# Transposes of two rows at once in even rows, strip transposes in odd rows, and the norm parameters in the transposes' PSUM banks

## The chip, the cores and the metric

The kernel runs on one core of a Trainium2 chip. The metric is the device time of one execution in microseconds. Before the change it was 2425.87 us, the median of three runs from 2424.24 to 2426.8.

## What is computed

The input is x, 8 images of 256 channels and 56 x 56 points, in fp32. There are two layers, each a block on a group norm of its input, added to that input:

```
# layer 0: involution
g   = group_norm(x)                                 # 32 groups of 8 channels
ker = w_span @ (w_reduce @ g + b_reduce) + b_span   # 16 groups x 49 taps per point
x   = x + sum over 49 taps of ker * patches7x7(g)   # 16 channels share a group's taps
# layer 1: two 3x3 convolutions with ternary weights, batch norms and relus
h   = relu(bn(conv(group_norm(x), tern(w1)) + centre term))
x   = x + relu(h + bn(conv(h, tern(w2)) + centre term))
```

The change lies in layer 0 alone.

## The kernel before

The program has four stretches: the involution, two convolutions (the function `conv_phase`, called twice) and a last pass that adds everything up. The involution is the function's part under `ph1`.

An image is cut into four **quarters** of 64 channels; the two halves of the partitions hold the upper and lower half of the image. A quarter has ten **rows** (`TY`), each of seven blocks of 3 x 8 points per half. The main loop (L811) goes over 32 quarters and the ten rows in each; `r = c * TY + ty` counts the 40 rows of an image.

TensorE does this in a row:

- `apply_row` (L690) multiplies patches by the quarter's tap matrices `a`: 56 matmuls into a PSUM tile `pa`. The patches are in a tile `q`, transposed, so that the points of a block lie on the partitions. Four of the seven block columns of `q` come by DMA from a DRAM buffer `xtd`, loaded four rows ahead by `prefetch`; three are made on the chip.
- `transpose_q` (L634) makes these three: three transposes from the padded image `xe` into a PSUM tile `ptq`, and a copy by ScalarE into `q` (L641). It runs two rows ahead (`QLEAD`).
- `generate` (L650) makes the next quarter's matrices in 14 **units**, one or two per row as `PER_ROW` says, none in the last row. A unit's matmuls `pg` go into a PSUM tile, ScalarE takes some of its planes (L675) and VectorE the rest (L680) into `a`.
- In every second row of a part of the image, `prep` (L582) makes a **strip** of the next image: GpSimd normalizes and spreads it into `xn` (L561), four transposes go into a PSUM tile `pt` (L605), ScalarE copies it to `stg` (L608), and DMAs store it to `xtd`. There are 16 strips per image. `xn` is one buffer.
- From row 20 on, `params` (L466) turns the next image's statistics into scale and shift: a matmul `gnp` with the group matrix (L146), a short chain on VectorE, a second matmul (L155), a longer chain with a square root on ScalarE (L158 to L161), and 16 small matmuls `br` (L478). It is a generator; the loop calls it once per row, and each `yield` ends a step.

`pick_out` (L710) then takes a row's result out of `pa`: ScalarE (L716), VectorE (L717), and GpSimd adds it to x (L720). VectorE also takes statistics of finished rows.

[...] The tag `ps`, two tiles of two banks, serves the units, the reduction `pk` (L538) and the parameters. The tags `pt` (transposes of both kinds) and `pa` have two tiles of one bank each. A tile goes back to its tag when its last reader is done.

The order of work on each engine is that of the program text: `pin` (L753) ties each instruction in the loop to the one before it on its engine. So a wait of one instruction holds up everything behind it on that engine. `transfer(2)` at the head of a row issues the strip's stores that are in `tasks`.

Of the kernel before, what the change touches and what calls it, by code (L numbers as in the profile page):

```python
# [7 lines left out]
F32 = mybir.dt.float32  # L8
# [7 lines left out]
P = 128  # L16
# [3 lines left out]
K, PAD, G = 7, 3, 16  # L20
KK = K * K
CR = C // 4
# [4 lines left out]
CH = P // 2  # L27
NCQ = C // CH
GQ = G // NCQ
GP = GQ // 2  # L30
HH = H // 2
# [3 lines left out]
TY, TX = 10, W // PX  # L35
# [15 lines left out]
SR = HH // 4  # L51
NSP = SR * QX
# [7 lines left out]
QLEAD = 2  # L60
# [18 lines left out]
def involution_tri_block_kernel(  # L79
# [3 lines left out]
    nc = tc.nc  # L83
# [57 lines left out]
    def group_norm_params(mv, dst, psum_tile, name):  # L141


        n = mv.shape[1]
        ps = psum_tile(f"gnp_{name}")
        nc.tensor.matmul(ps[:, :2 * n], grp_sb, mv.rearrange("p n s -> p (n s)"),  # L146
                         start=True, stop=True)
        yield
        gm = small.tile([P, n, 2], F32, tag=f"gn_gm{n}", name=f"gm_{name}")
        nc.vector.tensor_copy(gm.rearrange("p n s -> p (n s)"), ps[:, :2 * n])  # L150
        d = small.tile([P, n], F32, tag=f"gn_d{n}", name=f"d_{name}")
        nc.vector.tensor_tensor(d, mv[:, :, 0], gm[:, :, 0], ALU.subtract)
        nc.vector.tensor_tensor(d, d, d, ALU.mult)
        ps2 = psum_tile(f"gnp2_{name}")
        nc.tensor.matmul(ps2[:, :n], grp_sb, d, start=True, stop=True)  # L155
        yield
        var = small.tile([P, n], F32, tag=f"gn_var{n}", name=f"var_{name}")
        nc.vector.tensor_tensor(var, ps2[:, :n], gm[:, :, 1], ALU.add)  # L158
        rs = rstd_of(var, GN_EPS, name)
        nc.vector.tensor_copy(dst[:, :, 0], rs)  # L160
        nc.vector.scalar_tensor_tensor(dst[:, :, 1], gm[:, :, 0], -1.0, rs, ALU.mult, ALU.mult)  # L161
# [273 lines left out]
    with ExitStack() as ph1:  # L435
        ps_p = ph1.enter_context(tc.tile_pool(name="ps_p", bufs=2, space=PSUM))
        ps_a = ph1.enter_context(tc.tile_pool(name="ps_a", bufs=2, space=PSUM))

        def ps_tile(name):
            return ps_p.tile([P, 2, 512], F32, tag="ps", name=name)  # L440

        def ps_flat(name):
            return ps_tile(name).rearrange("p a f -> p (a f)")

# [21 lines left out]
        def params(b):  # L466


            dst = small.tile([P, NCQ, 2], F32, tag="gn1", name=f"gn1_{b}")
            yield from group_norm_params(mvs.pop(b), dst, ps_flat, f"a{b}")  # L470
            ps = ps_flat(f"br_{b}")
            for c in range(NCQ):
                nc.vector.tensor_scalar(
                    wrn[:, c, :].rearrange("p (i r) -> p i r", i=2),
                    wr[:, c, :].unsqueeze(1).to_broadcast([P, 2, CR]),
                    dst[:, c, 0:1], None, ALU.mult)
                for i in range(2):
                    nc.tensor.matmul(ps[i * CR:(i + 1) * CR, :1], wr[:CH, c, :], dst[:CH, c, 1:2],  # L478
                                     start=(c == 0), stop=(c == NCQ - 1))

            edge = small.tile([P, 2, NCQ], F32, tag="gn1e", name=f"gn1e_{b}")
            for j in range(2):
                nc.vector.tensor_scalar(edge[:, j], dst[:, :, 1], side_sb[:, j:j + 1], None, ALU.mult)
            prm[b], prm_edge[b] = dst, edge
            yield
            nc.vector.tensor_tensor(brn, br, ps[:, :1], ALU.add)

        gst1, mvs = {}, {}
# [13 lines left out]
        wr, wrn = fixed([P, NCQ, CR], "wr"), fixed([P, NCQ, 2 * CR], "wrn")  # L502
# [18 lines left out]
        for d in (d for ds in xt_d for d in ds):  # L521
            for r0, n in ((0, PAD), (PAD + HH, HQ - PAD - HH)):
                e = n * QX * RP // P
# [58 lines left out]
        def prep(b):  # L582

            for c in range(NCQ):
                d = xt_d[b % 2][c][:]

                def store(src, row, o=None, d=d):

                    n = src.shape[0]
                    if o is None:
                        src, to = src.rearrange("p k c -> p (k c)"), [[1, RP]]
                    else:
                        to = [[P, NK], [1, CH]]
                    nc.sync.dma_start(
                        bass.AP(d.tensor, d.offset + row * QX * RP + (o or 0), [[RP, n]] + to), src)

                for s in range(HH // SR):
                    spread(xn, xs[b, c][:, s * SR * W:(s + 1) * SR * W], 0, NK,  # L600
                           prm[b][:, c, 0:1], prm[b][:, c, 1:2])
                    yield
                    pt = ps_a.tile([P, 512], F32, tag="pt", name=f"pt_{b}_{c}_{s}")
                    for k in range(NK):
                        nc.tensor.transpose(pt[:NSP, k * P:(k + 1) * P],  # L605
                                            xn[:, k].rearrange("p r x -> p (r x)"), ident_sb)
                    stg = work.tile([P, NK, P], F32, tag="stg", name=f"stg_{b}_{c}_{s}")
                    nc.scalar.copy(stg[:NSP].rearrange("p k c -> p (k c)"), pt[:NSP, :RP])  # L608
                    tasks.append(lambda stg=stg, s=s: store(stg[:NSP], PAD + s * SR))

                    e = PAD * QX
                    if s == 0:
                        tasks.append(lambda stg=stg: store(stg[:e, :, CH:], PAD + HH, 0))
                    elif s == HH // SR - 1:
                        tasks.append(lambda stg=stg: store(stg[NSP - e:NSP, :, :CH], 0, CH))
                    yield


        tasks = []

        def transfer(n=1):
            while tasks and n:
                tasks.pop(0)()
                n -= 1
# [8 lines left out]

        def transpose_q(b, c, ty):  # L634

            pt = ps_a.tile([P, 512], F32, tag="pt", name=f"ptq_{b}_{c}_{ty}")
            for k in range(NX):
                nc.tensor.transpose(  # L638
                    pt[:NQ, k * P:(k + 1) * P],
                    xe[c % 2][:, k, PY * ty:PY * ty + QY].rearrange("p r x -> p (r x)"), ident_sb)  # L640
            nc.scalar.copy(loads[b, c, ty][:NQ, NK:].rearrange("p k c -> p (k c)"),  # L641
                           pt[:NQ, :NX * P])
# [134 lines left out]
            reduce(0, py)  # L777
        for _ in prep(0):
            transfer(len(tasks))
        apool = ph1.enter_context(tc.tile_pool(name="apool", bufs=1))  # L780

        def matrices(m):
# [14 lines left out]


        X_AT = (0, 1, 4, 5, 7, 8, 14, 15)
        STRIPS_AT = 23  # L800
        for _ in range(NQB):
            prefetch()
        for _ in surround(0, 0):
# [1 line left out]
        rows = [(b, c, ty) for b, c in quarters for ty in range(TY)]  # L805
        for k in rows[:QLEAD]:
            transpose_q(*k)
        pin(start=True)
        last = None
        strips = iter(())  # L810
        for m, (b, c) in enumerate(quarters):  # L811
            a = a_next
            gen = iter(())
            if m + 1 < len(quarters):
                a_next = matrices(m + 1)
                gen = generate(*quarters[m + 1], a_next)
                around = surround(*quarters[m + 1])
            more = b + 1 < B
            for ty in range(TY):
                r = c * TY + ty  # L820

                if last is not None and ty in (2, 3):
                    store_x1(*last, ty - 2)
                elif more and r in X_AT:
                    load_x(b + 1, X_AT.index(r) // 2, X_AT.index(r) % 2)
                transfer(2)

                row = apply_row(b, c, a, ty)
                prefetch()
                if m * TY + ty + QLEAD < len(rows):  # L830
                    transpose_q(*rows[m * TY + ty + QLEAD])

                if more and r >= 20:
                    if r == 20:
                        norm = params(b + 1)
                    next(norm, None)
                if ty == 1 and last is not None:
                    gn2_stats(*last, TY)
                elif ty >= 2:
                    gn2_stats(b, c, ty - 1)  # L840
                if more and 4 <= r < 20:
                    gn1_stats(b + 1, (r - 4) // NCB, (r - 4) % NCB)
                pick_out(b, c, ty, *row)
                for _ in range(PER_ROW[ty]):
                    next(gen, None)
                if more and r == STRIPS_AT:
                    strips = prep(b + 1)
                next(strips, None)
                if ty % 2 == 0 and m + 1 < len(quarters):
                    next(around)  # L850
                pin()
            for _ in gen:
                pass
            last = b, c
# [7 lines left out]
        for h in range(2):  # L862
            rows = slice(h * CH, (h + 1) * CH)
# [105 lines left out]
```

## Time and profile before

| | |
|---|---|
| time, median of three | 2425.87 us |
| profiled span | 2421.5 us |
| TensorE matmuls busy | 1885.9 us, 78% |
| VectorE busy | 1671.0 us, 69% |
| ScalarE busy | 1261.0 us, 52% |
| GpSimd busy | 592.9 us, 24% |
| first `pa` of the loop | at 184 us |
| transposes `ptq`, 960 | 178.6 us, mean 296 ns of one record |
| transposes `pt`, 512 | 88.9 us, mean 300 ns of one record |
| copies of `ptq` to `q`, 320 | 153.0 us, mean 478 ns |

In the profile's lines PE is TensorE, DVE VectorE, ACT ScalarE and POOL GpSimd. A line names the kernel's line, the operation, what it writes and reads, and in brackets how long the engine was idle before it and what ended the wait. Matmuls are pipelined: the time between two starts tells what one costs, and one record's length is more than that.

### The profile page before, as it was taken

The numbers are of one execution on the slowest core, as the hardware profiler recorded it, in microseconds if no ns is written. First come the engines' busy times: TensorE is split into PE (matmuls) and PEld (weight loads), VectorE is DVE, ScalarE is ACT, GpSimd is POOL, SyncE is SP. The second block draws the span as 40 slices with busy tenths as digits, with TensorE's granted clock in tenths as the row PEclk, the third lists the DMA queues.
The fourth block names the chain that finished last, engine by engine and source line by source line (L and its number), as shares of the span: only waits on it lengthen the run. The fifth ranks groups of instructions, "written<-read, shape, count | busy, mean of one in ns | idle before, by whom it ended". The sixth has DMA issues, their size and how long they took to land.

```text
span 2421.5 us, 72092 instructions
## 1 busy us (share of the span) xinstructions
PE 1885.9 (78%) x31080; PEld 1711.2 (71%) x31080; DVE 1671.0 (69%) x2570; ACT 1261.0 (52%) x2404; POOL 592.9 (24%) x1325
## 2 busy tenths in 40 slices
PE   3419898989899898989968999999499999980000
PEld 2217777777777777777858999999499999980000
DVE  6277465564746466574649999999599999974444
ACT  1105454545545454555645667666466677653333
POOL 2404463545546364554630000000000000000000
PEclk8559999999999999999988999999799999995555
DMA  4426363654636364553553233222432233229998
GB/s 155 152 99 177 106 198 109 182 151 144 187 110 206 90 198 137 160 173 107 161 185 149 109 132 137 112 109 106 176 123 109 109 136 136 109 111 430 430 430 377
DMA packets 124441, 406.46 MB, mean 168 GB/s; under 512 B 25694, under 2 KB 32220, under 8 KB 115420
## 3 DMA queue, kind: packets, MB, share of 16 engines
q1 hardware_dynamic: 117664, 360.89, 43.5%
q10 hardware_dynamic: 6460, 40.97, 4.2%
q8 instruction: 244, 4.00, 0.7%
q14 instruction: 73, 0.60, 0.1%
HBM read 259.33 MB, written 142.48 MB: 166 GB/s over the span
## 4 chain that ended last, share of the span: by engine, by line
PE 41%; DMA 10%; DVE 2%; ACT 1%; issue 1%; SPq 0%; POOL 0%; ACTq 0%; DVEq 0%
PE c L388 35%; DMA y1f<-y1d 3%; PE pg L671 3%; DMA out_y<-x1f 2%; DMA x1f<-x1d 2%; PE pa L704 2%; DVE x1f L899 1%; PE ptq L638 1%; DMA y2f<-y2d 1%; DMA y1d<-y 1%; DMA wq<-wqd 1%; PE pk L538 0%; PE pt L605 0%; ACT a L675 0%; DVE a L680 0%
## 5 line engine op out<-in xcount | busy, mean ns | idle before, releaser
L388 PE MATMUL c<-pl,wq 128*128 128x392 f32 x4608 | 857.3, 348 | 51.3 <-ACT pl L294 32.0
L388 PEld LDWEIGHTS c<-pl,wq 128*128 128x128 f32 x4608 | 855.4, 189 | 53.1 <-ACT pl L294 32.8
L680 DVE TENSOR_TENSOR a<-pg,bt 126x756 f32<-126x756 f32 (+3 forms) x640 | 393.8, 656 | 283.2 <-ACT a L675 225.7
L671 PE MATMUL pg<-kr,wl 64*126 64x140 f32 (+1 forms) x6144 | 460.9, 293 | 56.8 <-DVE a L680 32.5
L671 PEld LDWEIGHTS pg<-kr,wl 64*126 64x126 f32 x6144 | 394.8, 194 | 112.0 <-issue 70.3
L704 PE MATMUL pa<-a,q 126*32 126x48 f32 x17920 | 270.4, 208 | 71.5 <-DMA q<-xtd 44.5
L641 ACT COPY q<-ptq 126x384 f32<-126x384 f32 x320 | 153.0, 478 | 314.0 <-issue 171.0
L675 ACT ACTIVATE a<-pg,bt 126x126 f32<-126x126 f32 x768 | 242.5, 475 | 136.0 <-PE pg L671 136.0
L704 PEld LDWEIGHTS pa<-a,q 126*32 126x32 f32 x17920 | 221.7, 111 | 128.5 <-issue 89.4
L720 POOL TENSOR_TENSOR x<-x,inv 128x168 f32<-128x168 f32 x320 | 165.5, 517 | 577.4 <-DVE inv L717 557.0
L717 DVE SCALAR_TENSOR_TENSOR inv<-pa,half_sb,inv 128x168 f32<-128x168 f32 x320 | 118.6, 371 | 213.3 <-ACT inv L716 212.2
L294 ACT CAST pl<-r 128x812 fp32r<-128x812 f32 x192 | 162.4, 867 | 153.0 <-DVE r L289 136.4
L351 ACT ACTIVATE dummy<-y,nc 128x1568 f32<-128x1568 f32 x128 | 205.3, 1604 | 15.6 <-DVE y L374 14.3
L295 DVE TENSOR_TENSOR pl<-r,pl 128x812 fp32r<-128x812 f32 x192 | 186.3, 996 | 30.6 <-ACT pl L294 29.7
L275 POOL MEMSET xp<- 128x116 f32 x32 | 6.3, 196 | 817.7 <-DVE a L289 817.6
L561 POOL TENSOR_SCALAR xn<-x,gn 128x224 f32<-128x224 f32 (+2 forms) x384 | 184.2, 500 | 29.1 <-PE pt L605 18.5
L638 PE MATMUL ptq<-ident_sb,xe 128*126 128x128 f32 x960 | 178.6, 296 | 9.4 <-ACT stg L608 7.0
L561 POOL TENSOR_SCALAR xe<-x,gn 128x168 f32<-128x168 f32 (+2 forms) x384 | 160.3, 437 | 19.9 <-DVE gn L161 19.9
L139 DVE BATCH_NORM_STATS2 st<-x 128x6 f32<-128x392 f32 x256 | 138.0, 555 | 9.9 <-DMA x<-in_x 9.3
L608 ACT COPY stg<-pt 98x512 f32<-98x512 f32 x128 | 79.9, 624 | 122.0 <-PE pt L605 61.6
L716 ACT ACTIVATE inv<-pa,half_sb 128x168 f32<-128x168 f32 x320 | 126.9, 397 | 1.9 <-PE pa L704 1.8
L638 PEld LDWEIGHTS ptq<-ident_sb,xe 128*126 128x126 f32 x960 | 101.3, 143 | 29.7 <-ACT stg L608 7.2
(134 smaller groups left out, 1740.2 us busy)
## 6 DMA issues: line engine op xcount, KB each, us to landing
q<-xtd SPq DMA_DIRECT2D x320, 252.0 KB
raw<-x1d SPq DMA_DIRECT2D x32, 812.0 KB
raw<-y1d SPq DMA_DIRECT2D x32, 812.0 KB
x<-in_x SPq DMA_DIRECT2D x64, 392.0 KB
xtd<-stg SPq DMA_DIRECT2D x128, 196.0 KB
x1d<-x SPq DMA_DIRECT2D x64, 392.0 KB
y1d<-y SPq DMA_DIRECT2D x32, 784.0 KB
y2d<-y SPq DMA_DIRECT2D x32, 784.0 KB
```

Source lines behind the costliest of these rows:

```text
L294: nc.scalar.copy(hi, r)
L295: nc.vector.tensor_tensor(lo, r, hi.bitcast(F32), ALU.subtract)
L351: nc.scalar.activation(dummy, y[:, to], f, bias=shift[:, to:to + 1], accum_out=stats[:, to, j, n:n + 1])
L388: nc.tensor.matmul(ps[:, to, :NM], wq[:, k, t, dx, to * P:(to + 1) * P], part[:, t, :, dx:dx + W], start=(c == 0), stop=(c == last))
L561: nc.gpsimd.tensor_scalar(dst[:, i - d - k0:f - d - k0, :, x0:x0 + n], v[:, i:f, :, j0:j0 + n], scale, bias, ALU.mult, ALU.add)
L638: nc.tensor.transpose(pt[:NQ, k * P:(k + 1) * P], xe[c % 2][:, k, PY * ty:PY * ty + QY].rearrange("p r x -> p (r x)"), ident_sb)
L641: nc.scalar.copy(loads[b, c, ty][:NQ, NK:].rearrange("p k c -> p (k c)"), pt[:NQ, :NX * P])
L671: nc.tensor.matmul(dst, wl[rows, c, gp, o:o + NQ], kr[py][rows, px, :], start=True, stop=True)
L675: nc.scalar.activation(whole[:, g0 + i, p0 + j], ps[:NQ, i, j * nt:(j + 1) * nt], AF.Identity, bias=bt[:, c, g0 + i, p0 + j:p0 + j + 1])
L680: nc.vector.tensor_tensor(dst[:, g0:g0 + 2, p0:p0 + nv].rearrange("q g p t -> q g t p"), ps[:NQ, :, t0 * nv:t1 * nv].rearrange("q i (t p) ...
L704: nc.tensor.matmul(ps[o:o + 32, k * 2 * n:(k + 1) * 2 * n], q[:NQ, k, o:o + 32], av[:, t + k, g * 2 * n:(g + 1) * 2 * n], start=True, stop ...
L720: nc.gpsimd.tensor_tensor(xv, xv, iv.rearrange("p t (y x) -> p y t x", x=PX), ALU.add)
```

## The change

It changes the order of work in the loop and the places of some PSUM tiles; the instructions that compute stay the same in number.

- `transpose_q` runs in even rows only, for the rows two and three ahead, so that six transposes follow one another.
- Strips are stepped in odd rows only, right after `apply_row`; one step is the transposes of a strip, its copy, and the spread of the next strip. Before, a step was one of the two, at the end of each row.
- The parameters take one-bank tiles of the tag `pt` in place of two-bank tiles of `ps`, and are stepped twice per row: after the transposes and after `pick_out`. They have one more step: the second matmul and the `br` matmuls are each in a later step than the VectorE work that they need. A parameter tile is so given back in the row in which it is taken.
- `store` is bound when a strip's store is noted, since a store may now be issued after the generator has gone on to the next quarter; the first image's last stores are issued after the loop over `prep(0)`.

```diff
@@ group_norm_params
         nc.vector.tensor_tensor(d, d, d, ALU.mult)
+        yield
         ps2 = psum_tile(f"gnp2_{name}")
@@ ph1
+        def ps_one(name):
+            return ps_a.tile([P, 512], F32, tag="pt", name=name)
@@ params
-            yield from group_norm_params(mvs.pop(b), dst, ps_flat, f"a{b}")
-            ps = ps_flat(f"br_{b}")
+            yield from group_norm_params(mvs.pop(b), dst, ps_one, f"a{b}")
             for c in range(NCQ):
                 nc.vector.tensor_scalar(wrn ...)
-                for i in range(2):
-                    nc.tensor.matmul(ps ... br)
...
             prm[b], prm_edge[b] = dst, edge
+            yield
+            ps = ps_one(f"br_{b}")
+            for c in range(NCQ):
+                for i in range(2):
+                    nc.tensor.matmul(ps ... br)
             yield
@@ prep
-                    tasks.append(lambda stg=stg, s=s: store(stg[:NSP], PAD + s * SR))
+                    tasks.append(lambda stg=stg, s=s, store=store: store(stg[:NSP], PAD + s * SR))
...
-                    yield
@@ before the loop
         for _ in prep(0):
             transfer(len(tasks))
+        transfer(len(tasks))
...
-        STRIPS_AT = 23
+        PARAMS_AT, STRIPS_AT = 20, 23
@@ in the loop
                 row = apply_row(b, c, a, ty)
                 prefetch()
-                if m * TY + ty + QLEAD < len(rows):
-                    transpose_q(*rows[m * TY + ty + QLEAD])
-
-                if more and r >= 20:
-                    if r == 20:
-                        norm = params(b + 1)
-                    next(norm, None)
+
+                if more and r == PARAMS_AT:
+                    norm = params(b + 1)
+                if more and r == STRIPS_AT:
+                    strips = prep(b + 1)
+                if ty % 2:
+                    next(strips, None)
+                if ty % 2 == 0:
+                    for k in rows[m * TY + ty + QLEAD:m * TY + ty + QLEAD + 2]:
+                        transpose_q(*k)
+                next(norm, None)
+
...
                 pick_out(b, c, ty, *row)
+                next(norm, None)
                 for _ in range(PER_ROW[ty]):
                     next(gen, None)
-                if more and r == STRIPS_AT:
-                    strips = prep(b + 1)
-                next(strips, None)
```

More of the change, by code (lines that the diff above doesn't have):

```diff
@@ L476, in params @@
                     dst[:, c, 0:1], None, ALU.mult)
-                for i in range(2):
-                    nc.tensor.matmul(ps[i * CR:(i + 1) * CR, :1], wr[:CH, c, :], dst[:CH, c, 1:2],
-                                     start=(c == 0), stop=(c == NCQ - 1))
             edge = small.tile([P, 2, NCQ], F32, tag="gn1e", name=f"gn1e_{b}")
@@ L484, in params @@
             prm[b], prm_edge[b] = dst, edge
+            yield
+            ps = ps_one(f"br_{b}")
+            for c in range(NCQ):
+                for i in range(2):
+                    nc.tensor.matmul(ps[i * CR:(i + 1) * CR, :1], wr[:CH, c, :], dst[:CH, c, 1:2],
+                                     start=(c == 0), stop=(c == NCQ - 1))
             yield
@@ L602, in prep @@
                     yield
-                    pt = ps_a.tile([P, 512], F32, tag="pt", name=f"pt_{b}_{c}_{s}")
+                    pt = ps_one(f"pt_{b}_{c}_{s}")
                     for k in range(NK):
@@ L608, in prep @@
                     nc.scalar.copy(stg[:NSP].rearrange("p k c -> p (k c)"), pt[:NSP, :RP])
-                    tasks.append(lambda stg=stg, s=s: store(stg[:NSP], PAD + s * SR))
+                    tasks.append(lambda stg=stg, s=s, store=store: store(stg[:NSP], PAD + s * SR))
                     e = PAD * QX
                     if s == 0:
-                        tasks.append(lambda stg=stg: store(stg[:e, :, CH:], PAD + HH, 0))
+                        tasks.append(lambda stg=stg, store=store: store(stg[:e, :, CH:], PAD + HH, 0))
                     elif s == HH // SR - 1:
-                        tasks.append(lambda stg=stg: store(stg[NSP - e:NSP, :, :CH], 0, CH))
-                    yield
+                        tasks.append(lambda stg=stg, store=store: store(stg[NSP - e:NSP, :, :CH], 0, CH))
         tasks = []
@@ L634, in transpose_q @@
         def transpose_q(b, c, ty):
-            pt = ps_a.tile([P, 512], F32, tag="pt", name=f"ptq_{b}_{c}_{ty}")
+            pt = ps_one(f"ptq_{b}_{c}_{ty}")
             for k in range(NX):
@@ L809, in involution_tri_block_kernel @@
         last = None
-        strips = iter(())
+        strips = norm = iter(())
         for m, (b, c) in enumerate(quarters):
```

## The prediction

> **What bounds the kernel now.** I read the page first, for where the span goes, then TensorE's waits in the loop that is changed, then the order of time around the one place where they pile up.
>
> ```profile
> PE   3419898989899898989968999999499999980000
> ...
> PEclk8559999999999999999988999999799999995555
> ```
>
> A slice is 60.5 us. The loop over rows runs from slice 4 to slice 21, from 184 us (first `pa`) to about 1250 us. TensorE is busy at 8 to 9 tenths there and its clock is full, so TensorE is the bound; the convolutions behind it and the last pass are not touched. The waits of TensorE from 260 to 1240 us (columns: total us, times, longest):
>
> ```profile
> PE pg L671 <- DVE a L680: 20.7, 12, 2.1
> ...
> PE br L478 <- DVE gn L161: 12.5, 6, 2.1
> PE pa L704 <- DVE a L680: 8.7, 22, 0.8
> PE gnp_a L155 <- DVE d_a L153: 3.0, 5, 0.6
> ```
>
> Nothing here waits for a copy of transposes (`q`, `stg`): the transposes' two banks are no limit now. The waits that exist are of two kinds: 0.6 to 2.1 us, six times in this stretch (once per image: the norm parameters), and 0.2 to 0.8 us at 22 quarter ends. The order of time on TensorE around one image's parameters (start, us, what, idle before):
>
> ```profile
> 796.08 0.80 PE L704 MATMUL pa<-a,q 126*32 126x48 f32 x54 [0.77 <-DVE a L680]
> 796.81 0.55 PE L638 MATMUL ptq<-ident_sb,xe 128*126 128x128 f32 x3
> 797.19 0.29 PE L146 MATMUL gnp_a<-mv,grp_sb 128*128 128x8 f32 x2
> 797.41 0.98 PE L671 MATMUL pg<-kr,wl 64*126 64x140 f32 x12
> 799.79 0.98 PE L671 MATMUL pg<-kr,wl 64*126 64x140 f32 x12 [1.40 <-DVE a L680]
> ...
> 802.59 0.36 PE L155 MATMUL gnp_a<-d_a,grp_sb 128*128 128x4 f32 x2 [0.61 <-DVE d_a L153]
> ...
> 806.91 0.63 PE L478 MATMUL br<-gn,wr 64*64 64x1 f32 x16 [2.08 <-DVE gn L161]
> 807.47 1.15 PE L671 MATMUL pg<-kr,wl 64*126 64x126 f32 x16
> 810.67 2.07 PE L671 MATMUL pg<-kr,wl 64*126 64x126 f32 x16 [2.06 <-DVE a L680]
> 812.67 1.35 PE L704 MATMUL pa<-a,q 126*32 126x48 f32 x56
> 813.95 0.90 PE L638 MATMUL ptq<-ident_sb,xe 128*126 128x128 f32 x3
> 814.78 1.99 PE L671 MATMUL pg<-kr,wl 64*126 64x126 f32 x16
> ```
>
> Two things are to be seen. Four waits, 1.40 + 0.61 + 2.08 + 2.06 = 6.15 us, none in ordinary rows. And after the last the same instructions take nearly twice as long (`pg` x16 2.07 instead of 1.15, `pa` 1.35 instead of 0.80, `ptq` 0.90 instead of 0.55). By starts, excess 0.92 + 0.55 + 0.36 + 0.84 = 2.7 us. The same pattern stands at 242, 380, 519, 657, 937 and 1075 us. So an image's parameters cost about **8.8 us**, seven images 62 us.
>
> The two `pg` waits come from the banks of tag `ps`: a parameter tile keeps one of the two while it waits for VectorE in the next row, so the two units of that row share the other. The `br` wait is VectorE's chain (start, us):
>
> ```profile
> 804.39 0.15 DVE L158 TENSOR_TENSOR var_a<-gnp_a,gm_a 128x4 f32<-128x4 f32 x1
> ...
> 806.61 0.15 DVE L161 SCALAR_TENSOR_TENSOR gn<-gm_a,r_a 128x4 f32<-128x4 f32 x1
> 806.74 0.88 DVE L473 TENSOR_SCALAR wrn<-wr,gn 128x128 f32<-128x128 f32 x4
> ```
>
> [...] `var` stands behind the pick-out and evictions of its row. [...] here one record is 272 ns, but a run advances by 0.11 us each (x3 to the next `pg` 0.48 us, x4 0.57 us), and I use that pitch.
>
> **The change, part by part.**
>
> *Parameters out of the `ps` banks, in half-row steps.* The matmuls stay the same. I set zero at the end of `pa` in row 20 (796.81) and lay out the new order. Two rows' transposes 0.8; `gnp` needs a `pt` bank, and the first copy (0.62 us after the transposes start, 0.48 long) ends at 1.1: **new wait 0.2**, with the units of the row queued behind it. Units 0 and 1 run back to back to 3.0, since both `ps` banks are free: **the 1.40 is gone**. `gm` and `d` now sit in row 20 behind its pick-out, done at 3.0; row 21's `pa` ends at 3.7 and the second matmul finds `d`: **the 0.61 is gone**. Unit 2 waits about 0.1 for unit 0's eviction, moved back by the 0.55 of `gm`, `d`. VectorE then has evictions of units 0 and 1 (1.1 each, to 5.2), statistics 0.8, pick-out 0.4, then `var` to `gn`. That took 806.76 - 804.39 = 2.4 with 0.78 of waiting for ScalarE, where a copy stood ahead; now no copy does, so 1.9: `gn` at 8.4. TensorE, through with unit 2 at 4.8, `pa` 5.6 and six transposes 6.5, waits for it: **the `br` wait stays at about 2.0**. Behind it on TensorE are both units of row 22. `wrn` and `edge` (0.88 + 0.35) and unit 2's eviction 0.8 end at 10.5, and unit 4 needs that bank: wait 0.4 instead of 2.06. Row 23's `pa` ends at 12.3, against 813.95 - 796.81 = 17.1 before. Waits left: 0.2 + 0.1 + 2.0 + 0.4 = 2.7 of 8.8 with full clock, so 6.1 saved. One wait of 2 us may still halve the clock in some images; I take 1.2 us off: 4.9 x 7 = **34 us saved** (from 2.0 x 7 = 14, if chain and clock stay as bad, to 43).
>
> *Two rows' transposes at once.* As many transposes and copies. A group of three costs 0.48, six 0.48 + 3 x 0.11 = 0.81, so 0.15 less for two rows. The odd row then goes from `pa` to `pg` directly, which the trace never shows. At the cheap end it costs nothing, at the dear end 0.07, as the 0.11 pitch and the gap to the next form leave no more. So 0.08 to 0.15; I take 0.12. There are 160 pairs of rows, 24 of which end a quarter with a wait (three of four quarters; in the fourth `pk` hides it): 136 x 0.12 = **16 us saved** (11 to 20).
>
> *Quarter ends.* There TensorE waits for the last eviction into `a`, a fixed 1.84 us after row 8's last unit (0.60 `pa` + 0.47 `ptq` + 0.77 wait). Row 9's transposes, which lay in that gap, move ahead of row 8's units: 3 x 0.11 = 0.33 more before the gap, and the wait grows to 1.24: 24 x 0.33 = **8 us lost**. Some longer waits may halve the clock: 3 us lost (0 to 10).
>
> *Odd rows without strips.* A unit's bank comes free 2.1 us after its matmuls where ScalarE has two planes (793.1 to 795.2). Row 3 of a quarter reached it just in time; without its transposes it waits 0.4. In strip rows four transposes (0.57) fill that. About 11 rows have none: **4 us lost**.
>
> *Strips in odd rows.* Still 16 per image, the same instructions, moved from after the units to after `pa`. The store leaves with the next row, its copy done; its readers are four rows away or more, so no load gets later. The spread into `xn` now stands ahead of the pick-out's addition on GpSimd, which sat idle 485 us before that addition in this stretch; the statistics read it a row later. Zero, hidden by `pa` and units. The late binding of `store` and the flush after the first `prep` cost nothing: the first load waits 44.5 us for other transfers.
>
> Sum: 34 + 16 - 8 - 3 - 4 = 35 us. 2426 - 35 = **2391 us**.
>
> **The rivals.**
>
> *All waits vanish.* If VectorE comes sooner to `var` than I lay out, 62 + 16 - 8 = 70: 2356 us. For it: VectorE is idle a third of the loop. Against: the evictions of row 20 stand ahead in its queue. Chance 0.12.
>
> *VectorE's chain takes the place of the banks.* Only 1.40 + 0.61 are saved, 14 us for seven images, and the half clock stays: 14 + 16 - 8 - 3 - 4 = 15, so 2411 us. For it: `br` waits as before in my own layout. Against: the 2.06 wait has a cause that is removed. Chance 0.15.
>
> *Slower: the clock falls at quarter ends.* If the longer wait halves it at every second one, as at 810 us, 12 x 2.7 = 32 are lost, and the parameters, which follow such a quarter end, bring 20 instead of 34: 2426 + 32 + 8 + 4 - 20 - 16 = 2434 us. For it: at 381 us a 1.40 wait was followed by slow matmuls. Against: the same 1.40 was harmless in the other images shown. Chance 0.12.
>
> **How the numbers follow.** My forecast has 0.61. Its own ends are 2426 - (43 + 20 - 8) = 2371 and 2426 - (14 + 11 - 8 - 10 - 4) = 2423. The range 2368 to 2416 leaves out the far half of the first rival, the slow one, and the worst tail: about 0.2. Faster by over 0.2% (below 2421): the forecast, the first rival and most of the second, 0.81; within 0.2%: 0.06; slower 0.13.
>
> **What would show it.** In the profile after: `pg` waits on `a` for parameters gone, `gnp_a` L155 too; `br` waits near 2 us seven times; `pg` x16 records of 2.07 rarer; `pa` waits on `a` about 1.2 us at row 19 and 0.6 where strips run; `ptq` x6 of 0.81 us. I am wrong if `br` waits much more than 2 us, if slow matmuls follow quarter ends, or if transposes wait for `q` or `stg` copies.

## The result, and the profile after

The changed kernel takes 2367.66 us (median of four runs, 2361.05 to 2371.3) against 2425.05 us for the kernel before, whose median is now that of four runs too. The ratio of the times is 0.9761, with a 95% interval of 0.9736 to 0.9786. That is 57 us less where 35 were forecast, and 0.3 us below the range, which is far less than the 10 us over which the four runs spread. The direction and the parameters' part were right; the size of the whole was not.

All of it lies in the loop over rows. From the first `pa` to the last row's `pa` the trace has 1070.7 us before and 1018.3 us after; what stands ahead of the loop and behind it is the same within 1.1 us. The page's lines for TensorE and its clock, after:

```profile
PE   3418999999999989999959999999599999970000
...
PEclk8559999999999999999979999999799999985555
```

TensorE is still the bound. Its waits in the whole loop before, from 185 to 1255.4 us (total us, times, longest):

```profile
PE pg L671 <- DVE a L680: 24.5, 15, 2.1
PE pa L704 <- issue: 16.2, 16, 2.1
PE br L478 <- DVE gn L161: 14.6, 7, 2.1
PE pg L671 <- issue: 14.4, 18, 1.7
PE pa L704 <- DVE a L680: 10.2, 24, 0.8
...
PE ptq L638 <- issue: 2.4, 2, 1.3
```

And after, from 184 to 1202 us:

```profile
PE pa L708 <- DVE a L684: 21.9, 24, 1.4
PE pa L708 <- issue: 18.0, 23, 3.0
PE br L489 <- DVE gn L162: 10.7, 7, 1.6
...
PE pg L675 <- issue: 6.2, 10, 0.9
PE ptq L642 <- issue: 5.1, 6, 1.2
PE pg L675 <- DVE a L684: 2.5, 7, 0.5
PE gnp_a L146 <- ACT q L645: 2.0, 7, 0.3
```

`pg` waits on VectorE are nearly gone, the wait on the second group matmul is gone, `br` waits stay, and the quarters' ends wait twice as long. "issue" is time in which TensorE waited for nothing that the profile names: 33.0 us before, 29.5 after. The same place as before, an image's parameters, in the order of time on TensorE after:

```profile
633.00 0.80 PE L708 MATMUL pa<-a,q 126*32 126x48 f32 x54 [1.36 <-DVE a L684]
633.72 0.87 PE L642 MATMUL ptq<-ident_sb,xe 128*126 128x128 f32 x6
634.88 0.39 PE L146 MATMUL gnp_a<-mv,grp_sb 128*128 128x8 f32 x2 [0.29 <-ACT q L645]
635.20 1.70 PE L675 MATMUL pg<-kr,wl 64*126 64x140 f32 x24
636.83 0.80 PE L708 MATMUL pa<-a,q 126*32 126x48 f32 x56
637.56 0.38 PE L156 MATMUL gnp_a<-d_a,grp_sb 128*128 128x4 f32 x2
637.96 0.75 PE L675 MATMUL pg<-kr,wl 64*126 64x140 f32 x8
638.63 0.80 PE L708 MATMUL pa<-a,q 126*32 126x48 f32 x56
639.37 1.17 PE L642 MATMUL ptq<-ident_sb,xe 128*126 128x128 f32 x6
642.18 0.63 PE L489 MATMUL br<-gn,wr 64*64 64x1 f32 x16 [1.64 <-DVE gn L162]
642.74 3.24 PE L675 MATMUL pg<-kr,wl 64*126 64x126 f32 x32
645.90 1.34 PE L708 MATMUL pa<-a,q 126*32 126x48 f32 x56
```

Row 20's two units are one run (x24) and so are row 22's (x32): no bank is missing. `pg` x32 takes 3.24 us instead of the 2.03 of other rows, and the trace has the clock at 0.50 from 643.69 to 647.10 us: it still halves once here. Between 200 and 1180 us the trace has the clock at half for 58 us before and 27 us after. By the `pg` runs of 16 in the prediction, 2.07 us at half clock instead of 1.15, some 44% of such time is lost: by this estimate 26 us before and 12 after.

I then took the starts of all rows and compared two rows at a time. Rows 20 to 23, where the parameters are, take 163.6 us before (sum over eight images) and 129.1 after: 34.5 saved. All other rows together save some 18 us, where my other terms sum to 1. So the surplus is outside the parameters, and it is not the same in every row: pairs such as rows 26 and 27 or 28 and 29 save 1.3 and 1.4 us over the eight images, about the expected 0.15 each time, but rows 2 and 3, 12 and 13, and 34 and 35 save 4.7 to 5.0 us each.

### The profile page after: what moved, and what is told of

It reads as the page before. It is cut to its first block, busy times and chain, and to the rows that moved or that the text cites. A ratio compares the mean times of both kernels' runs of the same rounds, so it can differ in the third digit from the quotient of the medians.

```text
span 2367.9 us, 72166 instructions
## 1 busy us (share of the span) xinstructions
PE 1855.0 (78%) x31080; PEld 1705.5 (72%) x31080; DVE 1671.7 (71%) x2570; ACT 1255.0 (53%) x2404; POOL 590.8 (25%) x1325
## 3 DMA queue, kind: packets, MB, share of 16 engines
q8 instruction: 245, 4.01, 0.7%
## 4 chain that ended last, share of the span: by engine, by line
PE 72%; DMA 14%; DVE 7%; ACT 3%; issue 3%; POOL 1%; SPq 0%; ACTq 0%; DVEq 0%; POOLq 0%
PE c L389 36%; PE pg L675 16%; PE pa L708 9%; PE ptq L642 5%; PE pk L544 3%; DMA y1f<-y1d 3%; PE pt L610 3%; DMA out_y<-x1f 2%; DMA x1f<-x1d 2%; ACT a L679 2%; DVE a L684 2%; POOL xn L567 1%; DVE x1f L907 1%; DMA y2f<-y2d 1%; DMA y1d<-y 1%
## 5 line engine op out<-in xcount | busy, mean ns | idle before, releaser
L675 PE MATMUL pg<-kr,wl 64*126 64x140 f32 (+1 forms) x6144 | 449.7, 290 | 22.7 <-DVE a L684 9.8
L675 PEld LDWEIGHTS pg<-kr,wl 64*126 64x126 f32 x6144 | 387.3, 192 | 74.9 <-issue 40.1
L645 ACT COPY q<-ptq 126x384 f32<-126x384 f32 x320 | 138.6, 481 | 204.9 <-issue 73.2
L613 ACT COPY stg<-pt 98x512 f32<-98x512 f32 x128 | 75.0, 586 | 177.3 <-issue 80.4
L642 PE MATMUL ptq<-ident_sb,xe 128*126 128x128 f32 x960 | 145.1, 286 | 11.6 <-ACT stg L613 6.0
L888 ACT ACTIVATE xp<-raw,bi_bn,sc_bn 128x392 f32<-128x392 f32 (+1 forms) x128 | 84.8, 720 | 71.5 <-DVE a L290 57.1
```

Source lines behind the costliest of these rows:

```text
L642: nc.tensor.transpose(pt[:NQ, k * P:(k + 1) * P], xe[c % 2][:, k, PY * ty:PY * ty + QY].rearrange("p r x -> p (r x)"), ident_sb)
L675: nc.tensor.matmul(dst, wl[rows, c, gp, o:o + NQ], kr[py][rows, px, :], start=True, stop=True)
```

## The experiments

Each group of two or four kernels ran beside the kernel before; a ratio is that of a kernel's time to the kernel before in its group. The diffs are shortened to the lines that matter, and their comments are added. Where two kernels of different groups are compared, it is by their ratios.

**The two halves of the change alone, the strips' place, and the changed kernel again.**

> The changed kernel once more, unchanged, as the yardstick of this group. Both theories: 2367 us, within the 10 us that its four runs spread over (2361 to 2371).

Measured: 2360.43 us, ratio 0.9766 (0.9743 to 0.9788). Its loop took 1005.7 us in the trace, 12.6 less than in the first profile, with the same work: the issue waits were 22 us instead of 30. So two profiles of one kernel can differ by as much as a small change brings.

```diff
 # params_only: before.py with
+        yield                                  # in group_norm_params
-            yield from group_norm_params(mvs.pop(b), dst, ps_flat, f"a{b}")
+            yield from group_norm_params(mvs.pop(b), dst, ps_one, f"a{b}")
+            ps = ps_one(f"br_{b}")             # a step later
+                next(norm, None)               # after pick_out too
```

> The kernel before with the parameters' part alone: pt banks, half-row steps, the extra steps; transposes and strips as before. Theory A (the parameters' term of the prediction was right and the surplus lies in the pairing): rows 20 to 23 save 34.5 us in the trace, so about 2390 us (2385 to 2395). Theory B (the parameters bring the surplus too, because fewer halved clocks help rows behind them): 2375 us or less.

Measured: 2381.14 us, ratio 0.986 (0.9833 to 0.9886): 34 us less than before by the ratio, 39 by the two medians. In the trace rows 20 to 25 save 35.4 us, all other rows 5. Theory A on the parameters holds: the rows save what it says, though the median lies 4 us below its range.

```diff
 # pair_only: after.py with
-        yield                                  # in group_norm_params
+            yield from group_norm_params(mvs.pop(b), dst, ps_flat, f"a{b}")
+            ps = ps_flat(f"br_{b}")            # beside wrn
-                next(norm, None)               # after pick_out
```

> The changed kernel with the parameters as before (ps banks, one step per row); pairing and strips in odd rows stay. Theory A: the pairing brings what the parameters do not, 57 - 35 = 22 us, so about 2403 us (2398 to 2408), with run pairs of six transposes 0.80 us long and a wait of about 1.3 us at quarter ends without strips. The prediction's own terms (16 - 8 - 3 - 4 = 1 us): 2424 us. Theory B: 2415 us or more.

Measured: 2413.23 us, ratio 0.9972 (0.9961 to 0.9984): 7 us less than before, so neither 22 nor 1. Here the halves do not add: 34 to 39 and 7 make 41 to 46, together they bring 57. The trace shows where: outside rows 20 to 25 this kernel saves 30 us, but in rows 20 to 25 it loses 16.

```profile
652.45 0.80 PE L705 MATMUL pa<-a,q 126*32 126x48 f32 x54 [1.35 <-DVE a L681]
...
656.54 0.98 PE L672 MATMUL pg<-kr,wl 64*126 64x140 f32 x12 [1.46 <-DVE a L681]
...
659.34 0.36 PE L155 MATMUL gnp_a<-d_a,grp_sb 128*128 128x4 f32 x2 [1.08 <-DVE d_a L153]
...
664.05 0.63 PE L481 MATMUL br<-gn,wr 64*64 64x1 f32 x16 [2.14 <-DVE gn L161]
...
668.21 2.07 PE L672 MATMUL pg<-kr,wl 64*126 64x126 f32 x16 [2.05 <-DVE a L681]
```

The quarter's end now waits 1.35 us, and the parameters' old waits stand behind it, the second one 1.08 instead of 0.6. Half clock between 200 and 1180 us rises from 58 to 72 us, which by the same estimate accounts for about 6 of the 16 us; the rest is longer waits. So the parameters' half also removes what the pairing adds there.

```diff
 # strips_old: after.py with
-                if ty % 2:
-                    next(strips, None)         # after apply_row
+                next(strips, None)             # at the end of every row,
+                    yield                      # in two steps per strip
```

> The changed kernel with the strips where they stood before, a half step at the end of every row. Theory A (the strips' place costs nothing, they only fill TensorE elsewhere): 2368 us within 5. Rival (the strips in odd rows are what keeps the odd rows' units from waiting for their banks, a part of the surplus): 2375 us or more, with pg waits on VectorE in odd rows.

Measured: 2376.71 us, ratio 0.9843 (0.9818 to 0.9868), 16 us slower than the changed kernel beside it. So the strips' place is worth 16 us, which I had put at zero. But the rival's reason fails: `pg` waits on VectorE are 2.2 us, against 2.1 in the changed kernel of the same group. What grew has no name in the profile:

```profile
PE pa L710 <- issue: 18.6, 22, 2.2
...
PE ptq L644 <- issue: 10.4, 6, 2.8
...
PE pg L677 <- issue: 8.1, 11, 2.1
```

That is 37 us of issue waits in the loop against 22 in the changed kernel of the same group. It is not all: the profiled run is the slowest of this kernel's five (2388.16 us, 30.8 above the other profile), and in it the clock is at half for 51 us between 200 and 1180 us, against 24. By the same estimate half clock costs 12 of these 30.8 us, and a part of it follows long issue waits, such as one of 2.79 us.

**What the issue waits are.** A stretch of the kernel before, in order of time on TensorE:

```profile
355.70 0.37 PE L704 MATMUL pa<-a,q 126*32 126x48 f32 x14 [0.63 <-issue]
356.00 0.55 PE L638 MATMUL ptq<-ident_sb,xe 128*126 128x128 f32 x3
356.47 2.03 PE L671 MATMUL pg<-kr,wl 64*126 64x126 f32 x32
358.43 0.65 PE L605 MATMUL pt<-ident_sb,xn 128*98 128x128 f32 x4
359.01 0.80 PE L704 MATMUL pa<-a,q 126*32 126x48 f32 x56
359.74 0.55 PE L638 MATMUL ptq<-ident_sb,xe 128*126 128x128 f32 x3
360.22 1.14 PE L671 MATMUL pg<-kr,wl 64*126 64x126 f32 x15
362.51 0.37 PE L671 MATMUL pg<-kr,wl 64*126 64x126 f32 x1 [1.16 <-issue]
```

Count the matmuls from one wait to the next: 14 + 3 + 32 + 4 + 56 + 3 + 15 = 127, in the middle of runs. Each has a weight load (31080 of each in the whole trace), so that is 254 instructions. All 36 issue waits of this loop lie a multiple of 127 matmuls apart, give or take 4. The profile has a DMA queue q8, called "instruction": 4.01 MB in 245 packets, before and after, 16.4 KB each. Of these, 204 land in the loop, which has 26086 matmuls: one packet for 128 matmuls, every 5 us or so. And all 36 of these waits end 1.2 to 1.6 us after such a packet has landed, and all 40 in the first profile of the changed kernel 0.8 to 1.8 us after one. From this I take them for waits for instructions; the profile itself names no cause. Most packets go by without a wait: there are 28 to 40 waits to the 204 packets, 22 to 33 us in sum, in the kernel before and in the two profiles of the changed one. The next runs ask whether transfers hold the fetches up; the waits in their expectations are these issue waits.

```diff
 # strips_old_late: strips_old with
+                if ty % 2 == 0:
                     transfer(2)
 # odd_now: after.py with transfer(2) moved from the row's head to here
                 if ty % 2:
                     next(strips, None)
+                    transfer(2)
```

> Strips where they stood before, but their stores issued two rows later, at the head of the next even row, so that the DMA queue does not stand at a store that waits for its copy. Theory C (what the strips' place brings comes from when their stores go out: [...]): those waits fall from 35 us to about 23 and the ratio to before from 0.984 to about 0.978. Theory D (it is the place of the transposes on TensorE): no change, ratio 0.984.

Measured: 2382.15 us, ratio 0.9838 (0.9823 to 0.9853), issue waits 40 us. Theory C in this form fails: a store at the head of even rows, as in the changed kernel, is not enough. What theory D forecast, 0.984, is what came.

> The changed kernel with the strips' stores issued in the strip's own row, right after its copy is noted, so that the DMA queue waits for the copy again. Theory C: waits that no engine ends grow by 5 to 15 us, ratio to before about 0.981 to 0.984. Theory D: no change, ratio 0.977.

Measured: 2381.48 us, ratio 0.9831 (0.9812 to 0.985), issue waits 35 us. This one is as theory C has it, and theory D cannot explain it, since TensorE's order is unchanged. Neither theory alone fits both runs; that it depends on where the stores lie and on where TensorE is then would fit them, but is not shown.

**Without the strips' stores.**

```diff
-                transfer(2)
+                transfer(2) if m * TY + ty < 58 else tasks.clear()
```

> The changed kernel without the strips' stores from image 2 on (their patches are then left from images 0 and 1, so the result of those images is another one). Theory C2 (waits that no engine ends are instruction fetches held up by transfers, and the strips' stores are among these): these waits fall from 23 to 30 us to 15 or less, and the time by 8 us or more, ratio about 0.970 to 0.973. Theory E (the waits have nothing to do with transfers): no change, 0.976.

> Strips where they stood before, and without their stores from image 2 on (as in the run with the same left out of the changed kernel). Theory C2: without the stores the two places of the strips are equal: within 5 us of the other kernel without stores. Theory D (the transposes' place on TensorE costs 16 us by itself): still about 16 us slower than it.

> The kernel before without the strips' stores from image 2 on. If part of the change's gain is relief of the instruction fetch (theory C2), the kernel before gains more from leaving the stores out than the changed kernel did (5 permille, 0.976 to 0.971): waits that no engine ends from 35 to about 18 us, ratio about 0.990, so that between kernels without stores the change brings 0.971 / 0.990, about 46 us instead of 57. If the relief is no part of it: ratio about 0.995, and the change brings 57 us here too.

Measured: after_nostore 2351.80 us, ratio 0.9712 (0.9693 to 0.9731); strips_old_nostore 2353.23 us, 0.9725 (0.9708 to 0.9741); before_nostore 2391.78 us, 0.9884 (0.986 to 0.9907). The issue waits of after_nostore, 17 us:

```profile
PE pa L708 <- issue: 9.6, 13, 2.0
...
PE ptq L642 <- issue: 5.9, 6, 1.5
...
PE pg L675 <- issue: 1.6, 5, 0.6
```

And those of before_nostore, 15 us, where the kernel before has 33:

```profile
PE pa L704 <- issue: 8.8, 8, 2.3
...
PE pg L671 <- issue: 5.9, 9, 1.2
```

Without the stores 1.4 us lie between the two places of the strips, which is within the noise, where 16 lay between them. So the strips' new place gains nothing that can be seen on TensorE itself; it gains through transfers. The kernel before gains 1.2% from leaving the stores out, the changed one 0.5%; its issue waits stay a little above the 15 us of theory C2. The loop of before_nostore is 29.7 us shorter in the trace, and 18 of these are issue waits as the profile counts them. Between kernels without stores the change brings 0.9712 / 0.9884 = 0.9826, with the two intervals combined 0.980 to 0.986, about 42 us (35 to 50). So some 15 of the 57 us come from the transfers' side, a difference of two differences, uncertain by some 10 us. A direct count gives less: with stores the issue waits fall from 33.0 us to 29.5 in one profile of the changed kernel and to 22.2 in the other, so by 3.5 to 10.8; without stores they rise by 2.6, from 14.7 to 17.3.

**Banks or steps.**

```diff
 # steps_in_ps: params of after.py with ps_flat for ps_one
 # banks_only: params of before.py with ps_one for ps_flat, one next(norm) per row
```

> The changed kernel with the parameters' tiles back in the ps banks; half-row steps and extra steps stay, so a parameter tile is given back before the row's units need it. Theory A (the steps do the work, not the banks): no wait of 1.4 or 2.06 us on VectorE before pg, within 8 us of the changed kernel, ratio to before about 0.977. Theory B (the banks do it): the two pg waits are back, 24 us slower, ratio about 0.987.

Measured: 2376.18 us, ratio 0.9811 (0.9796 to 0.9825), 11 us slower than the changed kernel by ratio. `br` waits fall to 5.6 us, but `pg` waits 17.2 us on VectorE:

```profile
PE pg L675 <- DVE a L684: 17.2, 22, 1.3
...
PE br L489 <- DVE gn L162: 5.6, 7, 0.8
```

> The changed kernel with the parameters in the pt banks but stepped as before, once per row and without the extra steps. Theory A: br waits 2.1 us or more and the second group matmul 0.6 to 1.1 us, the clock halves as before the change, 20 us or more slower than the changed kernel, ratio about 0.985 to 0.99. Theory B (the banks do it): within 8 us of the changed kernel.

Measured: 2382.07 us, ratio 0.9835 (0.9818 to 0.9852), 17 us slower. `br` waits 15.0 us, the second group matmul 9.5, `pg` 3.5:

```profile
PE br L481 <- DVE gn L161: 15.0, 7, 2.1
PE gnp_a L155 <- DVE d_a L153: 9.5, 7, 1.4
...
PE pg L672 <- DVE a L681: 3.5, 8, 0.5
```

So neither alone is the cause: the banks take the `pg` waits; the steps, of which there are two more than before and not one (for the second group matmul and for `br`), take the other two. Each alone keeps most of the gain. In the traces the clock is at half for only 17 us (steps) and 24 us (banks) between 200 and 1180 us, 58 before.

**Two repairs that the profile after points to.**

```diff
 # quarter_end: after.py with
-                    for k in rows[at:at + 2]:             # in even rows
+                for k in rows[at:at + (2 if ty % 2 == 0 and ty < TY - 2 else ty >= TY - 2)]:
 # split_chain: params of after.py with its chain cut into
+            # row 21: var, sqrt; row 22: the rest to gn; row 23: wrn; row 24: edge, br, brn
```

> The changed kernel, but rows 8 and 9 of a quarter transpose one row each, so that row 9's three transposes lie in the wait at the quarter's end again. The prediction's term: 24 ends x 0.33 = 8 us, less 7 ends x 0.15 where nothing is waited for, so about 7 us faster, ratio 0.973; pa waits on VectorE's last eviction fall from 22 to about 10 us. Rival: the wait is hidden anyway or the instruction fetch takes it: no change.

Measured: 2356.52 us, ratio 0.9741 (0.9722 to 0.9759). `pa` waits on the last eviction fall from 22 to 11.1 us, as the term says. By ratio it is 5 us faster than the changed kernel beside which it was not run, and the intervals overlap, and its loop in the trace, 1006 us, is as long as that of the changed kernel's second profile; so the gain is likely and not shown.

> The changed kernel with the parameters' chain on VectorE spread over rows 21 to 24 and the br matmuls in row 24. Theory A: the br wait (1.64 us) goes, and with it most of the half clock behind it, about 1.5 us per image: 7 x 3 = 21 us faster at most, ratio about 0.968. Rival: the wait moves to the evictions that VectorE owes, or to the next wait: under 7 us faster.

Measured: 2351.76 us, ratio 0.9714 (0.9696 to 0.9732), 11 to 13 us faster than the changed kernel by ratio. Rows 22 and 23 take 52.8 us instead of 69 to 72, half clock between 200 and 1180 us is down to 10 us. A part goes back one row later, as the rival has it:

```profile
763.61 1.15 PE L708 MATMUL pg<-kr,wl 64*126 64x126 f32 x16 [1.21 <-DVE a L717]
...
766.58 0.63 PE L522 MATMUL br<-gn,wr 64*64 64x1 f32 x16 [0.29 <-ACT q L678]
```

The `br` wait is 0.29 us, on a copy of transposes; row 23's unit waits 1.21 us for an eviction. Rows 24 and 25 take 7 us more than before in sum.

> Both repairs in one kernel: VectorE's chain for the parameters spread over four rows, and row 9's transposes back in the quarter's end. If they add: 0.9714 less 2 permille, ratio about 0.969, 2347 us. If the waits that no engine ends take it back: 0.9714.

Measured: 2344.22 us, ratio 0.9684 (0.9664 to 0.9704). That is what adding forecasts, but the interval still touches that of split_chain alone. This kernel is 77 us faster than the kernel before and, by ratio, about 19 us faster than the changed one.

## Why the prediction was off, step by step

**Where it failed.** "The waits that exist are of two kinds" is the wrong sentence. The list from which I quoted the waits also had 29.3 us of issue waits in that stretch (14.4 on `pg`, 12.5 on `pa`, 2.4 on `ptq`); I left them out because no engine ended them, and no term of the sum could then change them. From that follows the second mistake, "Zero, hidden by `pa` and units" for the strips: no load came late for TensorE, but moving the strips moved their stores, and the issue waits depend on these (33 us in the kernel before, 15 without the stores). In their place the runs showed 16 us between the two places of the strips, and some 15 of the change's 57 us that are gone when no strips are stored. With the sizes below, about 11 of the 22 us by which I was off fall to this. The other 11 lie in terms that were in the sum and had the wrong size, above all the pairing; they follow one by one.

**The parameters: right.** Forecast 34. Rows 20 to 23 save 34.5, which holds 2 us of the pairing (14 x 0.15) and 4 us less for the longer quarter end in row 20 (7 x 0.58), so about 36 by itself. The waits: 1.40 and 0.61 gone, 2.06 gone (0.4 forecast), copy wait 0.29 (0.2 forecast), `br` 1.23 to 1.64 (2.0 forecast). What is left of them is 1.8 us per image where I had 2.7. The clock still halves for 3.4 us in six of the seven images, in one of them twice: 24 us, which by the estimate above cost 1.5 us per image where I had 1.2.

**Two rows at once: right in kind, too small.** Six transposes take 0.80 us to the next run, twice three take 0.95: 0.15 saved. The unknown step from `pa` to `pg` costs nothing (0.73 us from start to start, as to `ptq` before), the cheap end of my two. If all 160 pairs save it, that is 24 us, against my 136 x 0.12 = 16.

**Quarter ends: right for the wait.** `pa` waits on the last eviction went from 10.2 to 21.9 us, 11.7 for 24 ends, 0.49 each; the waits that I gave, 0.77 and 1.24, differ by 0.47. My term took only 0.33 of it, 8 us, since it let these pairs save nothing; here they are counted with the pairs above, so 12 us stand against it. The 3 us for the clock there, an estimate of mine, did not come: in the changed kernel no halved stretch follows a quarter end outside the parameters' rows.

**Odd rows without strips: too dear.** `pg` waits on VectorE are 2.5 us in the whole loop; I had 4 us.

So with these sizes the sum is 36 + 24 - 12 - 2 = 46, which is an estimate and 11 us more than I had. It stands against about 42 (35 to 50) measured between kernels without stores. The rest, about 11 us, I put down to the instruction fetch; the direct count of 3.5 to 10.8 us allows it and does not prove it.

**The rivals.** "All waits vanish" gave 2356 us and is 12 us from the result, nearer than my forecast, which is 23 us away. That is luck, since `br` waits did stay. Its reason is misread too: VectorE is idle for 41% of the loop before (584.6 us busy of the 995 from 185 to 1180), not for a third. In the second rival VectorE's chain did remain as a wait, but the half clock went down and did not stay. The slower clock at quarter ends came about in two images only, where the copy wait of 0.28 or 0.29 us followed one of 1.35 or 1.32.

**What stays open.** Which transfer holds up which fetch. strips_old_late and odd_now show that neither the stores' rows nor TensorE's order settles it, and the profile does not show when a fetch is asked for. The packets before the waits are not slow themselves (median 0.99 us in the kernel before, 1.03 for the others), so by my reading they began late, and why is not on record. The changed kernel itself differs by 12.6 us between two profiles with the same work. So what a reordering shows here can be luck of this kind, within some 15 us.

## What to carry to other kernels

Add up the waits on "issue" before forecasting a reordering of a long unrolled program: they are a term like the others, and a change that moves transfers can move them. To see what they are, count the matmuls between them. When two parts of a change touch waits of TensorE that lie near one another, try each alone: what one part adds can lengthen the other's waits and the time at half clock (72 us in pair_only, 58 before), so the parts need not add. And give a PSUM tile back in the step in which it is taken, while spreading the chain that feeds it over the rows, so that neither a bank nor the chain is waited for.

## What the runs showed of the hardware

- TensorE stood still on "issue" 28 times in the loop of after_again, 22 us in sum, and 43 times in that of strips_old_late, 40 us; the longest such wait was 3.3 us (quarter_end). In the kernel before there are 36, 33 us in sum: they lie multiples of 127 matmuls apart, give or take 4, and end 1.2 to 1.6 us after one of the 204 packets of the queue "instruction" that land in the loop. Leaving out the strips' stores of images 2 to 7 brought the 33 us to 15.
- Between 200 and 1180 us the clock stood at half in stretches of 3.41, 6.83 or 10.24 us: nine before, all eight after of 3.41 us. The single waits ahead of them were no longer than 2.1 us before and 3.0 us after: in the changed kernel one of 1.63 us, and in two images one of 1.32 or 1.35 us with 0.29 or 0.28 us close behind. The same waits left it at full in other images (1.64 us in the first; 1.36 and 0.29 us together). Waits of 1.32 and 1.33 us at quarter ends that stood alone did not halve it.
- A direct change from `pa` (weights of 126 x 32) to `pg` (64 x 126) took 0.73 us from `pa`'s start to the next start, and so did one from `pa` to transposes.
